# Splitting one inner token sum: the third raw row of T2 becomes an instruction of its own, placed just ahead of the other four rows

## The chip, the cores and the metric

The kernel runs on one core of a Trainium2 chip, in one launch. The metric is the device time of that core in microseconds, as the median over repeated executions. Five engines work side by side, each through its own queue in order: PE (TensorE, the matrix products), DVE (VectorE), ACT (ScalarE), POOL (GpSimd) and SP (SyncE, which here only issues DMAs). They wait for one another through semaphores.

## The reference, cut to what matters

Rows of 512 numbers (2 x 1024 of them) are normalized. A state-space convolution and a feed-forward net with low-rank additions are applied to the same normalized rows, and their product is added to the input. All numbers are float32.

```python
xn = layernorm(x)                                   # x: (2, 1024, 512)
s  = irfft(rfft(xn, 1024) * rfft(K, 1024))[..., :512] + D * xn
h1 = xn @ w1.T + 2 * (xn @ a1.T) @ b1.T             # hidden size 1376, rank 16
h3 = xn @ w3.T + 2 * (xn @ a3.T) @ b3.T
g  = silu(h1) * h3
f  = g @ w2.T + 2 * (g @ a2.T) @ b2.T
out = x + s * silu(f)
```

The change lies in the stage that makes h1 and h3, near its start.

## The kernel before, in words

**Tiling.** The 2048 tokens are cut into four blocks of 512, and a pair of blocks is a "sb" (there are NSB = 2). The products with w1 and w3 are done by a fast scheme with seven products in place of eight, applied twice: an outer level over quarters of the operands and an inner level over quarters of these. So 49 products of 128 x 128 by 128 x 512 make one pair of hidden chunks, and there are five pairs (NPAIR) and a remainder. The scheme wants sums of the operands. `outer_token_sum` makes the four outer sums T1 to T4 of the tokens for each sb into `xt`; the three quarters that enter unchanged stay in `xr`, the "raw" ones. `inner_token_sum` then makes the inner sums out of the raw quarters (3 rows of 512) and out of the outer sums (4 rows of 512). The inner T3 goes into tile `t_in[7]`, T2 into `t_in[6]`, T4 into `t_in[4]`, each with 7 rows: rows 0 to 2 raw, rows 3 to 6 from `xt`. T1 is made in place in `xr` and `xt`. All these sums are DVE work, with both inputs in SBUF. T3 is b22 - b12, T2 is T3 + b11, T4 is b21 - T2, so T2 needs T3 of the same rows.

**Who reads them.** A `Chain` is the run of seven inner-order products of one j (L766 on). Step i of chain j takes row `B_AT[i]` of the tile that belongs to j: T2's tile for j = 6, T3's tile for j = 7. The first chain with j = 6 stands at base 28 and takes its steps at the places `AT_T2`: step 1 (row 0) at 29.9, step 2 (row 1) at 33, step 6 (row 4) at 34.3, step 7 (row 5) at 34.8, step 5 (row 3) at 36.6, step 3 (row 2, the third raw row) at 39 and step 4 (row 6) at 43. `product` (L756) issues the matmuls; each float32 product of 512 columns stands as two MATMUL records in the trace. PE writes to four pairs of PSUM banks, `x`, `y`, `w` and `aux`. A bank is free again when ACT has copied it (L776, L794) or DVE has read it: L780 adds a `y` bank to a copy in SBUF, L870 adds a `x` or `w` bank to a running sum (`plus`). The same `plus` for the other half of the results, and the product of the gate (L837), run on POOL with all operands in SBUF. SP stores the finished gates to DRAM (L808).

**What sets the order.** Nothing is scheduled by a tool: the order is written out by hand. `at(place, what)` puts a call into a heap with a place; the heap is emptied in the order of the places (then in the order in which the calls came), and each call appends its instructions to its engine's queue. A place is about one product of 512 columns. `after(delay, what)` does the same relative to the place now being worked off. So a place decides what stands before what on each queue, and no more than that; the waits decide the times.

The list of inner token sums with their places stands at L1087 to L1098. The parameter `half` cuts a sum into two rows at a time and was used for T1 and T4 over `xt` only.

Of the kernel before, what the change touches and what calls it, by code (L numbers as in the profile page):

```python
# [107 lines left out]
def s4_gated_ffn(  # L108
# [107 lines left out]
    def at(place, what):  # L216
        heapq.heappush(events, (place, next(count), what))
# [116 lines left out]

    def inner_token_sum(name, raw, half=None):
        src, lo, n = (xr, 0, 3) if raw else (xt, 3, 4)
        some = slice(n) if half is None else slice(2 * half, 2 * half + 2)
        to = {i: t[:, lo : lo + n, :][:, some] for i, t in t_in.items()}
        b11, b21, b12_, b22 = (src[:, some, s, k, :] for s in range(2) for k in range(2))
        if name == 3:  # L340
            nc.vector.tensor_tensor(to[7], b22, b12_, sub)
        elif name == 2:
            nc.vector.tensor_tensor(to[6], to[7], b11, add)  # L343
        elif name == 4:
            nc.vector.tensor_tensor(to[4], b21, to[6], sub)
        else:
            nc.vector.tensor_tensor(b12_, b12_, b11, sub)
# [738 lines left out]
        at(when, lambda name=name: inner_weight_sum(w_pair[0], s_pair[0], name))  # L1086
    for name, raw, when, *half in (  # L1087
        (3, True, 21.6),
        (2, True, 22.8),
        (3, False, 24.2),  # L1090
        (2, False, 30.2),
        (1, True, 34.4),
        (1, False, 37.5, 0),
        (1, False, 40.3, 1),
        (4, True, 47.6),
        (4, False, 50.2, 0),
        (4, False, 52.3, 1),
    ):  # L1098
        at(when, lambda of=(name, raw, *half): inner_token_sum(*of))
# [495 lines left out]
```

## Time and profile before

| what | value |
|---|---|
| median of 3 runs | 442.54 us (442.51 to 442.62) |
| profiled execution | 442.84 us, of which the span is 441.0 us |
| mean granted TensorE clock | 0.998 |
| PE busy | 434.3 us, 98% of the span |
| DVE busy | 317.6 us, 72% |
| POOL busy | 207.9 us, 47% |
| ACT busy | 144.3 us, 33% |
| T2 raw (L343, 128x1536) | starts at 52.79 us, takes 2.64 us |
| T2 over `xt` (L343, 128x2048) | starts at 59.34 us, takes 2.27 us |

The span runs from the first to the last instruction; the profiled execution's time is 1.84 us longer than its span. A line of the timeline or of a group gives the engine, the line of the kernel, the operation, output<-inputs and shapes. "idle before <-" says what ended the engine's idle time. "PEld" is the load of weights into TensorE, which runs ahead of the product that needs it. A busy time includes time in which an instruction has started and is kept from its operands. On POOL the times are rough.

### The profile page before, as it was taken

What the parts mean: (1) busy time and instruction counts of PE and PEld (TensorE: products, weight loads), DVE (VectorE), ACT (ScalarE), POOL (GpSimd) and SP (SyncE); (2) the same over time, 40 slices, a digit from 0 to 9 for tenths busy, and PEclk for the clock granted to TensorE, in tenths of its full rate; (3) what the DMA queues carried; (4) which work ended last, traced back from release to release, by engine and by line L of the source; (5) the groups of instructions that cost most, each with busy time, mean ns of one, the idle gap of its engine ahead of it and who ended that gap; (6) DMA issues with size and microseconds to landing.
All of it is one profiled execution on the core that took longest, in us unless ns stands there. A gap on an engine that the chain in (4) does not pass through costs nothing.

```text
span 441.0 us, 5158 instructions
## 1 busy us (share of the span) xinstructions
PE 434.3 (98%) x1704; PEld 269.1 (61%) x1704; DVE 317.6 (72%) x536; ACT 144.3 (33%) x296; POOL 207.9 (47%) x156
## 2 busy tenths in 40 slices
PE   7999999999999999999999999999999999999996
PEld 7645334344444444444443446888898999999996
DVE  5899999954974687469745796979786885653234
ACT  2777242453255324532453242211101212212221
POOL 1416468895689368946894468400000122222221
PEclk9999999999999999999999999999999999999999
DMA  8931304025102500250035526395901832422211
GB/s 242 364 83 44 124 0 149 10 84 159 36 24 80 159 24 25 88 170 25 25 129 206 162 94 214 94 364 189 344 33 71 296 129 95 144 97 95 77 67 48
DMA packets 35467, 53.61 MB, mean 122 GB/s; under 512 B 4689, under 2 KB 21521, under 8 KB 35313
## 3 DMA queue, kind: packets, MB, share of 16 engines
q1 hardware_dynamic: 35088, 52.69, 36.3%
q10 hardware_dynamic: 352, 0.60, 0.4%
q8 instruction: 13, 0.21, 0.2%
q14 instruction: 14, 0.11, 0.1%
HBM read 33.88 MB, written 19.40 MB: 121 GB/s over the span
## 4 chain that ended last, share of the span: by engine, by line
PE 86%; DVE 7%; DMA 2%; ACT 2%; issue 1%; POOL 0%; SPq 0%; DVEq 0%; ACTq 0%; POOLq 0%
PE x L756 43%; PE y L756 22%; PE w L756 11%; PE aux L930 4%; PE w L930 2%; DMA s<-in_x_dram 1%; DVE xt L328 1%; DVE s L453 1%; DVE w L441 1%; DMA w<-in_w1T_dram 1%; PE y L529 1%; PE aux L711 1%; DVE t_in L343 1%; ACT c L254 1%; DVE aux L1310 1%
## 5 line engine op out<-in xcount | busy, mean ns | idle before, releaser
L1313 POOL TENSOR_TENSOR o<-o,xin 128x512 f32<-128x512 f32 (+1 forms) x17 | 23.3, 1369 | 133.0 <-DVE o L1312 133.0
L837 POOL TENSOR_TENSOR s<-c,s 128x512 f32<-128x512 f32 (+1 forms) x44 | 63.2, 1442 | 17.6 <-ACT c L829 12.4
L776 ACT COPY s<-x 128x512 f32<-128x512 f32 (+1 forms) x54 | 31.5, 584 | 84.5 <-PE x L756 84.4
L756 PE MATMUL x<-t_in,s 128*128 128x512 f32 (+1 forms) x148 | 55.4, 501 | 0.0
L870 POOL TENSOR_TENSOR s<-ua_three,s 128x512 f32<-128x512 f32 x20 | 35.9, 1793 | 25.4 <-DVE s L780 25.4
L780 DVE TENSOR_TENSOR s<-s,y 128x512 f32<-128x512 f32 (+1 forms) x54 | 36.0, 679 | 15.7 <-PE y L756 10.6
L756 PEld LDWEIGHTS x<-t_in,s 128*128 128x128 f32 x148 | 26.6, 190 | 23.3 <-issue 11.7
L870 POOL TENSOR_TENSOR ua_three<-ua_three,s 128x512 f32<-128x512 f32 x20 | 30.6, 1529 | 13.8 <-DVE s L780 13.8
L756 PE MATMUL y<-t_in,s 128*128 128x256 f32 (+1 forms) x108 | 35.9, 459 | 0.1
L1335 ACT COPY z<-x 128x256 f32<-128x256 f32 x24 | 8.8, 371 | 70.5 <-PE x L756 70.4
L870 POOL TENSOR_TENSOR s<-u_three,s 128x512 f32<-128x512 f32 x20 | 29.4, 1474 | 1.8 <-ACT c L829 1.0
L1310 DVE TENSOR_TENSOR aux<-aux,m 128x384 f32<-128x384 f32 x32 | 18.1, 565 | 15.8 <-PE aux L930 14.3
L829 ACT ACTIVATE c<-c 128x512 f32<-128x512 f32 x40 | 25.2, 632 | 12.9 <-DVE c L870 12.9
L756 PEld LDWEIGHTS y<-t_in,s 128*128 128x128 f32 x108 | 20.1, 190 | 11.6 <-issue 8.1
L794 ACT COPY w<-x 128x512 f32<-128x512 f32 (+1 forms) x37 | 21.1, 570 | 11.6 <-PE x L756 11.5
L870 POOL TENSOR_TENSOR u_three<-ua_three,u_three 128x512 f32<-128x512 f32 x10 | 15.6, 1556 | 13.4 <-DVE u_three L780 13.3
L756 PE MATMUL x<-t_in,w 128*128 128x512 f32 x40 | 21.0, 605 | 0.0
L756 PE MATMUL x<-xt,w 128*128 128x512 f32 x40 | 20.7, 598 | 0.0
L756 PE MATMUL x<-xr,w 128*128 128x512 f32 x40 | 20.6, 614 | 0.0
L756 PE MATMUL x<-xr,s 128*128 128x512 f32 x40 | 20.5, 614 | 0.0
L756 PE MATMUL x<-xt,s 128*128 128x512 f32 x40 | 20.4, 592 | 0.0
L756 PE MATMUL y<-xt,w 128*128 128x512 f32 x40 | 19.8, 592 | 0.0
(302 smaller groups left out, 908.7 us busy)
## 6 DMA issues: line engine op xcount, KB each, us to landing
g_dram<-s SPq DMA_DIRECT2D x40, 256.0 KB, 2.1
g<-g_dram SPq DMA_DIRECT2D x10, 512.0 KB, 5.8
xin<-in_x_dram SPq DMA_DIRECT2D x16, 256.0 KB, 2.7
out_dram<-o SPq DMA_DIRECT2D x14, 256.0 KB, 2.0
t_in<-g_dram SPq DMA_DIRECT2D x6, 512.0 KB, 4.1
w<-in_w1T_dram SPq DMA_DIRECT2D x10, 256.0 KB, 3.6
w<-in_w3T_dram SPq DMA_DIRECT2D x10, 256.0 KB, 4.9
t_in<-in_x_dram SPq DMA_DIRECT2D x8, 256.0 KB, 5.7
```

The lines of the kernel that those rows point to most:

```text
L254: nc.scalar.activation(value("c"), x_in[b][tt], AF.Copy, accum_out=sums_of_x[b][:, 0, tt : tt + 1])
L756: nc.tensor.matmul(ps[:, cols], lhsT=lhsT, rhs=rhs if parts == 1 else rhs[:, cols], start=first and i == 0 and part == 0, stop=i == len(pa ...
L776: nc.scalar.copy(t, self.x)
L780: nc.vector.tensor_tensor(t, t, self.y, add)
L794: nc.scalar.copy(self.w, self.x)
L829: nc.scalar.activation(c, c if src is None else src, AF.Silu)
L837: nc.gpsimd.tensor_tensor(g, act, g, mult)
L870: (nc.vector if o < 20 else nc.gpsimd).tensor_tensor(to, a, b, add)
L930: nc.tensor.matmul(to[:, n * P : (n + 1) * P], lhsT=x_, rhs=by, start=start, stop=True, skip_group_check=True,)
L1310: nc.vector.tensor_tensor(y[:, P:], y[:, P:], m[:, n * P : (n + 3) * P], add)
L1313: (nc.vector if last else nc.gpsimd).tensor_tensor(o, o, self.xin[h][:, cols], add)
L1335: nc.scalar.copy(t, xb)
```

## The change

The T2 sum of the raw rows was one DVE instruction over rows 0 to 2 (128x1536) at place 22.8. It is now two: rows 0 and 1 (128x1024) at 22.8 and row 2 (128x512) at 30.1, ahead of T2 over `xt` (rows 3 to 6) at 30.2. `half` is bounded so that the second half of three rows is one row.

```diff
     def inner_token_sum(name, raw, half=None):
         src, lo, n = (xr, 0, 3) if raw else (xt, 3, 4)
-        some = slice(n) if half is None else slice(2 * half, 2 * half + 2)
+        some = slice(n) if half is None else slice(2 * half, min(2 * half + 2, n))
         to = {i: t[:, lo : lo + n, :][:, some] for i, t in t_in.items()}
...
     for name, raw, when, *half in (
         (3, True, 21.6),
-        (2, True, 22.8),
+        (2, True, 22.8, 0),
         (3, False, 24.2),
+        (2, True, 30.1, 1),
         (2, False, 30.2),
         (1, True, 34.4),
```

On DVE's queue the order around it was and is:

| before | after |
|---|---|
| T3 raw, 128x1536 (L341) | T3 raw, 128x1536 |
| T2 raw, 128x1536 (L343) | T2 raw rows 0 and 1, 128x1024 |
| c<-ua_one,x (L870) | c<-ua_one,x |
| T3 over xt, 128x2048 (L341) | T3 over xt, 128x2048 |
| s<-s,y 128x512 (L780) | s<-s,y 128x512 |
| | T2 raw row 2, 128x512 |
| s<-s,y 96x512 (L780) | s<-s,y 96x512 |
| T2 over xt, 128x2048 (L343) | T2 over xt, 128x2048 |
| s<-w, 128x896 (L453) | s<-w, 128x896 |

The order on PE, ACT, POOL and SP is the same in both kernels.

## The prediction

> **What bounds the kernel now.** I read the share of each engine first (PE busy for 98% of the span, so it bounds the whole), then the chain of work that ended last around the change, then the timelines of DVE, POOL and PE there. A mean hides stages; the chain, in order of time, shows who set the pace here:
>
> ```profile
> 52.79 2.64 DVE t_in L343
> 55.42 0.61 DVE c L870
> ...
> 57.27 1.96 PE x L756 x4
> ```
>
> Up to 56.03 the chain is DVE, with the instruction that is split in it (2.64 us); two short steps of ACT follow, and from 57.27 PE carries it. DVE's own timeline, with the neighbours of the split instruction:
>
> ```profile
> 50.94 1.74 DVE L341 TENSOR_TENSOR t_in<-xr 128x1536 f32<-128x1536 f32 x1
> 52.79 2.64 DVE L343 TENSOR_TENSOR t_in<-t_in,xr 128x1536 f32<-128x1536 f32 x1
> 55.35 0.67 DVE L870 TENSOR_TENSOR c<-ua_one,x 128x512 f32<-128x512 f32 x1
> 55.95 2.28 DVE L341 TENSOR_TENSOR t_in<-xt 128x2048 f32<-128x2048 f32 x1
> 58.15 1.27 DVE L780 TENSOR_TENSOR s<-s,y 128x512 f32<-128x512 f32 x2
> 59.34 2.27 DVE L343 TENSOR_TENSOR t_in<-t_in,xt 128x2048 f32<-128x2048 f32 x1
> ```
>
> There is no gap over 0.11 us from 50.94 to 61.61: DVE is full (busy 6.00 of 6.00 us from 56 to 62). So T2 over xt, last of the list, ends when all the work ahead of it is done, in whatever order. POOL, at the same time:
>
> ```profile
> 48.69 5.12 POOL L870 TENSOR_TENSOR s<-ua_three,s 128x512 f32<-128x512 f32 x1 [6.04 <-DVE s L780]
> 58.90 4.86 POOL L870 TENSOR_TENSOR s<-ua_three,s 128x512 f32<-128x512 f32 x1 [5.09 <-DVE s L780]
> ...
> 73.46 1.27 POOL L870 TENSOR_TENSOR u_three<-ua_three,u_three 128x512 f32<-128x512 f32 x1
> ```
>
> The same operation takes 1.27 us alone and about 5 beside DVE's sums with both inputs in SBUF; DVE pays too, when POOL is in first: T2 raw took 2.64 us and T3 raw, of the same size, 1.74, so 0.90 of it was a wait until POOL's operation ended (48.69 + 5.12 = 53.81). I call that a collision. Last, PE:
>
> ```profile
> 56.08 1.13 PE L756 MATMUL x<-t_in,s 128*128 128x512 f32 x2
> 57.27 1.96 PE L756 MATMUL x<-xr,last 128*96 128x512 f32 x4
> 59.06 1.02 PE L756 MATMUL w<-t_in,s 128*128 128x512 f32 x2
> 59.92 1.88 PE L756 MATMUL y<-xt,last 128*96 128x512 f32 x4
> 61.67 1.12 PE L756 MATMUL x<-t_in,s 128*128 128x512 f32 x2
> 62.64 0.59 PE L756 MATMUL y<-t_in,s 128*128 128x512 f32 x1
> ```
>
> A product (two passes) takes 0.86 us from start to start (59.06 to 59.92). From 54.26 to 62.64 there are nine, 7.74 us, in 8.38: PE lost 0.64 us, at 56.08 (weights waited for c L870, which frees an x bank), at 57.27 (for ACT's copy, behind the silu of that c) and at 61.67 (for T2 over xt). Later, from 81.69 to 87.42, six products (5.16 us) took 5.73: another 0.57, again behind DVE (c L870 at 81.91, then L780). These two numbers, 1.21 together, are what PE can win here.
>
> **The change, part by part.**
>
> *The first piece.* Row to row, 512 elements more cost (2.28 - 0.67) / 3 = 0.54 us. The piece of 1024 starts at 52.79 behind the same T3 raw and the same POOL operation, so I keep the collision of 0.90: 2.64 - 0.54 = 2.10, ending 0.54 earlier. Bounds: 1.21 without a collision (as L345 128x1024 at 82.51), 2.64 if all is lost again. c L870, T3 over xt and the first L780 move up 0.54 with it; the products that these read ended before 52, so nothing new holds them. PE gains at 56.08 and 57.27 what those two waits cost, some 0.5 of the 0.64.
>
> *The piece that is moved.* Row 2 alone stands after that L780, at 58.15 - 0.54 = 57.61 + 0.60 = 58.21, and takes 0.67, with the next start 0.60 later (58.15 to 58.75). Between ends far apart, 0.6 and 0.6 + a collision of up to 1.74 (below), I take 0.60: what it overwrites in its tile POOL and PE had done with before T3 raw began, and POOL's next operation is released by the L780 just ahead, so it starts 0.1 behind this piece. What is queued behind it: the 96x512 L780 at 58.75 becomes 58.81 (+0.06, the fixed cost of one more instruction: 0.60 - 0.54). That L780 must end before PE may add to its y bank at 59.92: PE had its weights loading at 59.49, right as it ended (59.42). So PE's 0.5 is taken back to about 0.3 already here. The reader of row 2, step 3 of the chain, comes after steps 6, 7 and 5, all of which need T2 over xt, so the later row delays nobody. No DMA, and nothing on PE, ACT, POOL or SP, changes its place.
>
> *T2 over xt.* It starts at 59.41 instead of 59.34. Does it collide? Before, POOL's operation was released by the L780 at 58.15 and started at 58.90; T2 still ran in 2.27, without a collision, and POOL waited (4.86). After, POOL starts at about 58.37, while row 2 holds DVE; when row 2 ends at 58.81 the PSUM-reading L780 runs, and POOL can take its turn. The nearest rows are these:
>
> ```profile
> 78.10 1.08 DVE L453 TENSOR_TENSOR s<-w 128x896 f32<-128x896 f32 x1
> 79.10 0.67 DVE L780 TENSOR_TENSOR s<-s,y 128x512 f32<-128x512 f32 x1
> 79.70 1.69 DVE L345 TENSOR_TENSOR t_in<-xt,t_in 128x1024 f32<-128x1024 f32 x1
> ...
> 82.51 1.21 DVE L345 TENSOR_TENSOR t_in<-xt,t_in 128x1024 f32<-128x1024 f32 x1
> ```
>
> SBUF sum, L780, SBUF sum, with POOL's operation started at 78.32 inside the first: the second sum took 1.69 for 1.21, a collision of 0.48. I take 0.48: T2 takes 2.75, ends at 62.16 instead of 61.61, and PE's product of 61.67 starts at 62.22: +0.55, all earlier gain gone. Bounds: no collision, +0.06; the largest in the stretch, L347 128x1024 at 69.31, 2.95 for 1.21, so 1.74: +1.80.
>
> The Trainium skill, SBUF — State Buffer, "Who interferes with whom", says that a DVE instruction with two SBUF inputs and a GpSimd instruction that reads SBUF exclude each other, and that whichever issues first keeps the pair for the whole instruction. The 0.90 and 0.48 agree; the row at 59.34 does not by its start, since POOL's record begins 0.44 earlier and yet T2 ran free. By the rule the split opens a turn for POOL, and the sum is +0.55 at 62 us; by the row at 59.34 it is +0.06.
>
> *What becomes of the 0.55.* DVE stays full until 72.2, so it carries the 0.55 on. At 75.28 the raw T4 (L345 128x1536) took 2.29 for 1.74, waiting 0.55 for the POOL operation of 74.69 (end 75.95). POOL paces itself there (73.46, 74.69 back to back), so DVE coming 0.55 later finds it over: DVE is back at its old times from 77.5 on, but for some hundredths. PE, 0.55 late, then reaches 81.69 to 87.42, where it used to lose 0.57 to DVE, and loses nothing. Cover: this wait. Without it 0.55 stays. From 92 on DVE is idle for two thirds (3.44 us busy of 92 to 102), and PE carries the chain again.
>
> Sum on the profiled execution: +0.55 at 62, -0.49 to -0.55 by 87, so +0.00 to +0.06 on 442.84 (span 441.0 plus 1.84 around it). The median, 442.54, is 0.30 lower than that execution; the same step gives 442.6.
>
> **The rivals.**
>
> *B, DVE keeps its turn.* As at 59.34: no collision, T2 over xt only 0.06 later, everything after as before: 442.6. It differs in the trace, not in the time.
>
> *C, the 0.55 is not given back.* POOL's operations at 73.46 and 74.69 wait for L780s that are 0.55 late too; if they slide along, L345 collides as before, and PE keeps +0.55 to +0.61: 443.1. Against it: POOL was still waiting its turn when these L780s ended.
>
> *D, slower: POOL takes two turns.* At 69.31 L347 waited while two POOL operations passed. If L837, queued behind L870, passes ahead of T2 over xt as well, the collision is 1.74: PE +1.80 at 62, L345 gives back 0.55, leaving 1.25: 443.8. It decides from a collision of 0.88 + 0.55 - 0.06 = 1.37 on. Against it: that L837 reads what the L870 ahead writes, so it must wait for its end and leaves a gap to DVE.
>
> *E, faster: the collisions fall away.* If the shorter first piece is not held by POOL (0.90 of 2.64), DVE is up to 1.4 earlier from 54 on, T2 over xt can end ahead of PE, and so can c L870 and the L780s at 82 to 87: all of the 1.21, 441.3. Against it: POOL then takes its turn behind the piece, at c L870, and T3 over xt pays.
>
> **How the numbers follow.** My forecast (A, 0.48; 442.3 to 443.0 by itself) is 442.6. B 0.10, C 0.10, D 0.20, E 0.12: D and E get more than their arguments alone, since who is first is decided by tenths of a microsecond and every later turn hangs on it. 0.2% is 0.885 us, about what a measurement of this kernel can tell from no change. A, B and C lie within it (0.68), less 0.02 of A on each side: same 0.64, slower 0.22, faster 0.14. The range reaches up to D, 443.8, and down to 441.9, short of E; about 0.17 is left out.
>
> **What would show it.** L343 128x1024 about 2.1 us; c L870 at 54.8; L343 128x512 near 58.2, 0.67 long; POOL's L870 starting near 58.4 and lasting about 1.7 instead of 4.86; T2 over xt 2.75 us (2.27 says B, over 3.6 says D); PE's product behind it at 62.2; L345 128x1536 shorter than 2.29 (unchanged says C); the PE waits near 82 to 87 smaller. I am wrong if the shift at 62 differs from the shift at 100 by something other than these two, or if blocks behind 130 us, whose order did not change, run differently.

## The result and the profile after

| | median | lowest to highest | executions |
|---|---|---|---|
| before | 442.27 us | 441.78 to 442.88 | 13 |
| after | 443.61 us | 442.35 to 444.87 | 13 |

The ratio is 1.0028, with a 95% interval of 1.0018 to 1.0039. The kernel became slower by about 0.3%; the interval excludes no change, and its lower end, 0.18%, lies just under the prediction's bound of 0.2%. 443.61 lies inside the predicted range (441.9 to 443.8), but the likeliest single time was 442.6, no change, and "slower" had a chance of 0.22.

The profiled execution of the changed kernel took 443.06 us, with a span of 441.3 us and a mean granted clock of 0.999 (before: 442.84, 441.0, 0.998). Up to 54 us its instructions stand 0.15 us earlier than those of before, because the start of the span fell otherwise (PE's product of 54.26 is at 54.11). All shifts below have this 0.15 taken out; the shift of that product is what is taken out for the other kernels too. A "turn" of POOL below is one operation of POOL that goes between two sums of DVE while DVE's next sum, already started, stands still.

DVE's timeline of the changed kernel (start, duration, engine, line, operation, shapes, idle time before):

```profile
52.63 2.10 DVE L343 TENSOR_TENSOR t_in<-t_in,xr 128x1024 f32<-128x1024 f32 x1
54.66 0.67 DVE L870 TENSOR_TENSOR c<-ua_one,x 128x512 f32<-128x512 f32 x1
55.26 2.28 DVE L341 TENSOR_TENSOR t_in<-xt 128x2048 f32<-128x2048 f32 x1
57.46 0.67 DVE L780 TENSOR_TENSOR s<-s,y 128x512 f32<-128x512 f32 x1
58.06 0.68 DVE L343 TENSOR_TENSOR t_in<-t_in,xr 128x512 f32<-128x512 f32 x1
58.66 0.67 DVE L780 TENSOR_TENSOR s<-s,y 96x512 f32<-96x512 f32 x1
59.26 2.76 DVE L343 TENSOR_TENSOR t_in<-t_in,xt 128x2048 f32<-128x2048 f32 x1
61.94 2.15 DVE L453 TENSOR_TENSOR s<-w 128x896 f32<-128x896 f32 x1
...
70.76 1.74 DVE L347 TENSOR_TENSOR xt<-xt 128x1024 f32<-128x1024 f32 x1
...
74.90 0.69 DVE L870 TENSOR_TENSOR ua_one<-ua_one,w 128x512 f32<-128x512 f32 x1 [0.61 <-PE w L756]
...
76.10 1.75 DVE L345 TENSOR_TENSOR t_in<-xr,t_in 128x1536 f32<-128x1536 f32 x1
```

The first piece takes 2.10 us, row 2 0.68, T2 over `xt` 2.76: as forecast to 0.01. The line that the forecast lacks is the next one: the weight sum of L453 takes 2.15 us, where it took 1.07 before at 61.55. The rows of the kernel before to set beside these:

```profile
61.55 1.07 DVE L453 TENSOR_TENSOR s<-w 128x896 f32<-128x896 f32 x1
...
69.31 2.95 DVE L347 TENSOR_TENSOR xt<-xt 128x1024 f32<-128x1024 f32 x1
...
75.28 2.29 DVE L345 TENSOR_TENSOR t_in<-xr,t_in 128x1536 f32<-128x1536 f32 x1
```

POOL's timeline of the changed kernel says why:

```profile
58.21 1.65 POOL L870 TENSOR_TENSOR s<-ua_three,s 128x512 f32<-128x512 f32 x1 [4.56 <-DVE s L780]
59.95 10.23 POOL L837 TENSOR_TENSOR s<-c,s 128x512 f32<-128x512 f32 x4
```

Its L870 takes 1.65 us instead of 4.86 (the turn that costs T2 over `xt` 0.48), so the L837 queued behind it is ready at 59.95, in the middle of T2 over `xt`. When T2 ends, L837 goes next and L453 stands for 1.08 us. (The experiment without POOL's turns, below, tests this reading.)

POOL does not take more of DVE than before; it takes it earlier. What the sums of DVE lose to POOL between 58 and 78 us, each against the same shape without a collision:

| DVE's sum | before | after |
|---|---|---|
| T2 over xt (2.27) | 0 | 0.49 |
| L453 128x896 (1.07) | 0 | 1.08 |
| L347 128x1536 (1.75) | 0.48 | 0.47 |
| L347 128x1024, first (1.21) | 0.48 | 0.48 |
| L347 128x1024, second (1.21) | 1.74 | 0.53 |
| L345 128x1536 (1.74) | 0.55 | 0.01 |
| sum | 3.25 | 3.06 |

Two turns have moved from 69 to 76 us, where no product is waiting for DVE, to 59 to 63 us, where PE is. In DVE's timeline above, L347 at 70.76 (1.74 us instead of 2.95) and L345 at 76.10 (1.75 instead of 2.29) are the turns that are gone there, and at 74.90 DVE waits 0.61 us for PE: from there on DVE is late only because PE is. It is 0.97 late at 76.10 like PE, and 0.42 late from 77.77 on, since L345 no longer collides. PE's timeline of the changed kernel, around 62 us and then around 85 us:

```profile
62.07 1.13 PE L756 MATMUL x<-t_in,s 128*128 128x512 f32 x2 [0.73 <-DVE t_in L343]
63.04 1.02 PE L756 MATMUL y<-t_in,s 128*128 128x512 f32 x2
64.24 1.95 PE L756 MATMUL x<-t_in,s 128*128 128x512 f32 x4 [0.18 <-DVE s L453]
```

```profile
82.50 1.02 PE L756 MATMUL x<-xt,s 128*128 128x512 f32 x2
83.36 1.02 PE L756 MATMUL x<-t_in,w 128*128 128x512 f32 x2
84.22 1.10 PE L756 MATMUL x<-xr,s 128*128 128x512 f32 x2
...
86.88 1.02 PE L756 MATMUL y<-t_in,w 128*128 128x512 f32 x2
87.74 1.02 PE L756 MATMUL y<-xt,s 128*128 128x512 f32 x2
```

And the same five products in the kernel before:

```profile
81.69 1.02 PE L756 MATMUL x<-xt,s 128*128 128x512 f32 x2
82.64 1.13 PE L756 MATMUL x<-t_in,w 128*128 128x512 f32 x2
83.77 1.12 PE L756 MATMUL x<-xr,s 128*128 128x512 f32 x2
...
86.45 1.12 PE L756 MATMUL y<-t_in,w 128*128 128x512 f32 x2
87.42 1.02 PE L756 MATMUL y<-xt,s 128*128 128x512 f32 x2
```

PE is 0.55 us late at 62.07 (62.07 - 61.67 + 0.15) and, after the wait for L453, 0.97 late from 65 to 82.50. The 0.57 that the kernel before lost between 81.69 and 87.42 is nearly all gone (5.24 us for the six products instead of 5.73), so at 87.74 PE is 0.48 late. It stays at 0.48 up to 105 us. This +0.48 is what the change does to the schedule; the engines' times up to 100 us repeat to 0.03 in a second profile of the same kernel.

Behind 100 us single profiles scatter. There, a load of weights from DRAM may end the chain (the shift falls to 0.11 at 107 us only because the kernel before lost 0.36 there in its profile). The experiments go into both parts.

### The profile page after: what moved, and what is told of

The parts are those of the page before. It is cut to its first block, busy times and chain, and to the rows that moved or that the text cites. A ratio compares the mean times of both kernels' runs of the same rounds, so it can differ in the third digit from the quotient of the medians.

```text
span 441.3 us, 5159 instructions
## 1 busy us (share of the span) xinstructions
PE 434.2 (98%) x1704; PEld 269.4 (61%) x1704; DVE 317.2 (72%) x537; ACT 144.4 (33%) x296; POOL 206.6 (47%) x156
## 4 chain that ended last, share of the span: by engine, by line
PE 85%; DVE 9%; ACT 2%; issue 2%; DMA 1%; POOL 0%; SPq 0%; DVEq 0%; POOLq 0%
PE x L756 43%; PE y L756 22%; PE w L756 11%; PE aux L930 4%; PE w L930 2%; DVE s L453 1%; DVE t_in L343 1%; DMA s<-in_x_dram 1%; DVE xt L328 1%; DVE t_in L341 1%; DVE w L441 1%; PE y L383 1%; PE y L529 1%; PE aux L711 1%; ACT c L254 1%
## 5 line engine op out<-in xcount | busy, mean ns | idle before, releaser
L837 POOL TENSOR_TENSOR s<-c,s 128x512 f32<-128x512 f32 (+1 forms) x44 | 66.1, 1508 | 16.7 <-ACT c L829 11.5
L780 DVE TENSOR_TENSOR s<-s,y 128x512 f32<-128x512 f32 (+1 forms) x54 | 36.0, 678 | 15.8 <-PE y L756 10.6
L870 POOL TENSOR_TENSOR s<-ua_three,s 128x512 f32<-128x512 f32 x20 | 32.7, 1634 | 25.1 <-DVE s L780 25.1
L870 POOL TENSOR_TENSOR ua_three<-ua_three,s 128x512 f32<-128x512 f32 x20 | 29.6, 1481 | 13.8 <-DVE s L780 13.8
L870 POOL TENSOR_TENSOR s<-u_three,s 128x512 f32<-128x512 f32 x20 | 29.4, 1473 | 1.8 <-ACT c L829 1.0
L870 POOL TENSOR_TENSOR u_three<-ua_three,u_three 128x512 f32<-128x512 f32 x10 | 15.6, 1556 | 15.8 <-DVE u_three L780 14.0
L756 PE MATMUL y<-xt,s 128*128 128x512 f32 x40 | 19.8, 592 | 0.0
```

The source lines that it names most:

```text
L756: nc.tensor.matmul(ps[:, cols], lhsT=lhsT, rhs=rhs if parts == 1 else rhs[:, cols], start=first and i == 0 and part == 0, stop=i == len(pa ...
L780: nc.vector.tensor_tensor(t, t, self.y, add)
L837: nc.gpsimd.tensor_tensor(g, act, g, mult)
L870: (nc.vector if o < 20 else nc.gpsimd).tensor_tensor(to, a, b, add)
```

## The experiments

Theory A: the loss is two turns of POOL that the new order brings forward, at T2 over `xt` and at L453. Rival X: one more instruction, standing at its own place, costs by itself. Rival Y: the loss comes from the load of weights near 101 us. In the shift table PE's starts stand against the kernel before, with the shift of the product at 54.26 taken out (us; the column heads are times in the kernel before):

| kernel | 58.2 | 62.6 | 64.8 | 87.0 | 105.2 |
|---|---|---|---|---|---|
| after | -0.46 | +0.55 | +0.97 | +0.48 | +0.48 |
| after again | -0.46 | +0.58 | +0.99 | +0.50 | +0.50 |
| split only | +0.09 | +0.09 | +0.09 | +0.10 | +0.10 |
| row 2 early | -0.46 | +0.09 | +0.09 | +0.10 | +0.10 |
| row 2 late | -0.46 | -0.51 | +0.52 | +0.03 | +0.04 |
| row 2 between | -0.46 | +1.16 | +1.16 | +0.67 | +0.67 |

**The same kernel again.**

> The changed kernel once more, with its profile, to see another execution of it. Theory A (turns): row 2 ends while GpSimd's addition is waiting, GpSimd takes the turn, T2 over xt takes 2.7 to 2.8 us, GpSimd takes the next turn ahead of s<-w (L453), which takes about 2.1 us instead of 1.07, and TensorE is 0.5 us late at 62 us and more after 64 us; how much of it is given back by 92 us differs from execution to execution. Time +0.2 to +0.4% against the kernel before. Rival X (the extra instruction itself costs): T2 over xt back at 2.27 us and the time as late all the same. Rival Y (a weight load from DRAM near 101 us): TensorE no later than before at 92 us and later behind 103 us.

443.12 us (442.12 to 444.38, 12 executions) against 442.52 (35) on the same chip: ratio 1.0015 (1.0003 to 1.0028). T2 over `xt` takes 2.76 and L453 2.15 again. So it is slower by 0.15 to 0.28%, on both sides of the bound of 0.2%. PE is 0.50 late at 87 and at 105 us, ahead of what waits for the load, so rival Y does not explain the schedule's part. The profiled execution was one of the long ones, 444.22 us, and its chain of waits shows where the rest was lost, in two stretches:

```profile
100.63 0.40 SPq L402
101.03 0.05 issue
101.08 4.96 DMA w<-in_w1T_dram
...
106.17 0.70 DVE w L393
106.87 0.04 issue
106.91 1.12 PE y L756 x2
...
228.83 9.31 DMA w_a<-in_w2T_dram
```

The load of w1 took 4.96 us (3.45 in the profile before), L393 waited for it, and PE for L393: PE lost 1.00 us there, and its shift goes from 0.50 to 1.13 (the kernel before lost 0.36 at the same place). The load of w2 took 9.31 us (8.46 to 8.91 in the other profiles), and the shift goes to 1.68. At 301 us it grows by another 0.2, behind a wait for DVE.

**The split alone.** Row 2 directly behind rows 0 and 1:

```diff
-        (2, True, 30.1, 1),
+        (2, True, 22.81, 1),
```

> Row 2 is split off but stands right behind rows 0 and 1 (place 22.81). Theory A: the two pieces follow each other without a turn for GpSimd, T2 over xt keeps 2.27 us, everything from there on is 0.07 us later, so the time is 0.0 to +0.1 us. Rival X: as late as the change, +1.0 to +1.5 us. Rival Y: no statement, unless the load near 101 us moves.

442.39 us (441.75 to 443.87, 12), ratio 0.9998 (0.9987 to 1.0008). DVE's timeline of it:

```profile
58.95 2.28 DVE L343 TENSOR_TENSOR t_in<-t_in,xt 128x2048 f32<-128x2048 f32 x1
61.15 1.08 DVE L453 TENSOR_TENSOR s<-w 128x896 f32<-128x896 f32 x1
```

The additional instruction costs PE 0.09 us and no measurable time. No turn of POOL falls at T2 over `xt` or at L453.

**The move, but to an earlier place**, behind T3 over `xt` and ahead of the first L780:

```diff
-        (2, True, 30.1, 1),
+        (2, True, 24.3, 1),
```

> Row 2 stands behind T3 over xt (place 24.3), ahead of the L780 that releases GpSimd, so GpSimd starts in the PSUM-reading L780 as before and not in an SBUF sum. c<-ua_one,x still moves up by 0.54 us. Theory A: T2 over xt keeps 2.27 us, 0.07 us later than before; time 0.0 to +0.1 us. Rival X: +1.0 to +1.5 us. If moving c<-ua_one,x up does harm by itself, +1.0 us or more with T2 over xt at 2.27 us.

442.47 us (442.06 to 443.23, 12), ratio 0.9996 (0.9988 to 1.0005). Here c L870 and T3 over `xt` come 0.52 earlier, about as in the changed kernel (PE -0.46 at 58.2), row 2 stands by itself, and T2 over `xt` takes 2.28 and L453 1.08. Rival X falls with these two runs: split and moved apart, the row costs nothing as long as POOL's turns stay where they were.

**The move to a later place**, behind T2 over `xt`:

```diff
-        (2, True, 30.1, 1),
+        (2, True, 30.25, 1),
```

> Row 2 stands behind T2 over xt (place 30.25), its reader comes later still. Theory A: GpSimd's start falls in the second L780 as before, T2 over xt keeps 2.27 us and ends 0.5 us earlier than before, TensorE's product behind it starts about 0.4 us earlier, and from s<-w (L453) on everything on VectorE is 0.07 us later, which by 87 us sets TensorE again: time -0.1 to +0.1 us. Rival X: +1.0 to +1.5 us.

442.30 us (441.75 to 443.87, 12), ratio 0.9994 (0.9983 to 1.0005). T2 over `xt` is free, as expected, but a turn falls on row 2 behind it, which was not expected; DVE's timeline:

```profile
58.35 2.28 DVE L343 TENSOR_TENSOR t_in<-t_in,xt 128x2048 f32<-128x2048 f32 x1
60.56 1.76 DVE L343 TENSOR_TENSOR t_in<-t_in,xr 128x512 f32<-128x512 f32 x1
62.25 1.08 DVE L453 TENSOR_TENSOR s<-w 128x896 f32<-128x896 f32 x1
```

One turn (1.08 us) makes PE 0.52 late at 65 us, and PE gives back 0.49 of it by 87: what the prediction said of one turn, nearly to the hundredth (+0.03).

**Two neighbours of the changed kernel exchanged**, so that row 2 stands between the second L780 and T2 over `xt`:

```diff
-        (2, True, 30.1, 1),
+        (2, True, 30.15, 1),
```

> The changed kernel with two neighbours on DVE exchanged: row 2 behind the second L780 (96x512) instead of ahead of it, so the order is L780, L780, row 2, T2 over xt. Theory A (what decides is when POOL's L870 gets its first turn, and so where the turn of L837 falls): POOL waits inside the second L780 as before; either it gets no turn until T2 over xt and L453 are done (T2 over xt 2.27, L453 1.07, PE at 86 us +0.0 to +0.1, ratio 1.000), or it gets one at row 2 (row 2 about 1.75, T2 over xt free, PE +0.55 at 62, no second turn at L453 unless L837 is ready by its end; at 86 us 0.0 to +0.5). Rival X (a row of its own at this place costs by itself): as the changed kernel, PE +0.48 at 86 us, ratio 1.002 to 1.003.

442.75 us (442.20 to 443.18, 11) against 442.21 (21): ratio 1.0007 (0.9998 to 1.0016). DVE's timeline:

```profile
58.38 1.77 DVE L343 TENSOR_TENSOR t_in<-t_in,xr 128x512 f32<-128x512 f32 x1
60.07 2.28 DVE L343 TENSOR_TENSOR t_in<-t_in,xt 128x2048 f32<-128x2048 f32 x1
62.27 1.08 DVE L453 TENSOR_TENSOR s<-w 128x896 f32<-128x896 f32 x1
```

POOL gets a full turn at row 2 (1.77 for 0.68, so 1.09), and none at T2 over `xt` or L453. PE waits 1.49 us for T2 and is 1.16 late:

```profile
62.40 1.12 PE L756 MATMUL x<-t_in,s 128*128 128x512 f32 x2 [1.49 <-DVE t_in L343]
```

The 1.77 was expected, the 1.16 not: I had added a turn of 0.48 for PE, where a row of 1.77 means one of 1.09, and 0.06 + 1.09 is the 1.15 measured to 0.01. The give-back is again 0.49, which leaves +0.67. So one turn can cost PE more than the two of the changed kernel, if all of it falls on the sum that PE waits for next.

**POOL's turns taken away, in both kernels.** The five operations of POOL from 58 to 71 us work on 16 of 512 columns; the rest of these additions and gate products is left out, so only the schedules are compared, one profile of each:

```diff
-                    nc.gpsimd.tensor_tensor(g, act, g, mult)
+                    n = 16 if 25 < now[0] < 38 else TB
+                    nc.gpsimd.tensor_tensor(g[:, :n], act[:, :n], g[:, :n], mult)
...
+            if o >= 20 and 25 < now[0] < 38:
+                to, a, b = to[:, :16], a[:, :16], b[:, :16]
```

> The kernel before, with POOL's five operations of this stretch (the L870 addition on s and the gate products of L837 from 58 to 71 us) done on 16 of their 512 columns, so that POOL hardly takes a turn; the rest of those additions and products is left out, and its time is that of a kernel that leaves them out. It is the base for after_small_pool, profile against profile. Every theory: T2 over xt 2.27 us, s<-w L453 behind it 1.07, L347 128x1024 about 1.21 in place of 2.95, so DVE up to 1.7 us earlier from 70 us on and PE's waits from 82 to 87 us smaller than before's 0.57.

> The changed kernel with the same five POOL operations on 16 of 512 columns (the same part left out). Theory A (the loss is two turns that POOL takes at T2 over xt and at L453): both turns gone, T2 over xt 2.27 to 2.35, L453 1.07 to 1.15, and PE at 64 us and at 86 us within 0.1 us of before_small_pool. Rival X (the extra instruction and the new order of DVE cost by themselves, whatever POOL does): PE still 0.4 us or more behind before_small_pool at 64 and at 86 us.

DVE's timeline of the changed kernel with the small operations (L873 is the L870 of the other kernels):

```profile
58.79 2.28 DVE L343 TENSOR_TENSOR t_in<-t_in,xt 128x2048 f32<-128x2048 f32 x1
60.99 1.08 DVE L453 TENSOR_TENSOR s<-w 128x896 f32<-128x896 f32 x1
61.99 0.68 DVE L873 TENSOR_TENSOR ua_one<-ua_one,w 128x512 f32<-128x512 f32 x1
62.59 1.75 DVE L347 TENSOR_TENSOR xr<-xr 128x1536 f32<-128x1536 f32 x1
```

Both turns are gone. PE's shift against the kernel before is +0.07 at 65 us and -0.42 at 87 for this one, +0.01 and -0.47 for its base, so the change is worth +0.06 and +0.05 between the two. That is theory A's number, and the fixed cost of one instruction; rival X wanted 0.4 or more. The base shows besides what POOL's turns cost the kernel before in this stretch: 0.47 us by 87 us (441.96 and 441.51 us were the single times of the two).

**The loss near 85 us, taken away alone.** In the kernel before, the next pair's first weight sum (L453 at 78.10) is put later:

```diff
-                (3, ready(7) + 1.2),
+                (3, ready(7) + (14 if c == 0 else 1.2)),
```

> The kernel before with one other instruction moved: the next pair's first weight sum (L453 128x896 at 78.10 us, 1.0 us of DVE) goes behind 92 us, where DVE is idle for two thirds. If PE's loss of 0.57 us from 81.69 to 87.42 is DVE being late there, as the prediction has it, PE is 0.4 to 0.57 us earlier at 87 us and the time is 442.0, ratio 0.9985 to 0.999. If that loss comes from elsewhere (ACT, or the banks themselves), PE is unchanged at 87 us and the ratio 1.000. The sums that follow s7 come later with it; if PE then waits for them behind 95 us, the gain is lost there.

PE's timeline of it, where the kernel before needs 5.73 us for the six products:

```profile
81.13 1.02 PE L756 MATMUL x<-xt,s 128*128 128x512 f32 x2
81.99 1.02 PE L756 MATMUL x<-t_in,w 128*128 128x512 f32 x2
...
86.37 1.02 PE L756 MATMUL y<-xt,s 128*128 128x512 f32 x2
```

It needs 5.24, and PE is 0.47 us earlier: that loss is DVE being late, as the prediction had it. The gain does not last. 443.17 us (442.75 to 443.73, 11), ratio 1.0019 (1.0010 to 1.0029): slower, where 442.0 was expected. By 96 us 0.30 of the 0.47 is gone, and I read that from the timeline as the later weight sums standing ahead of the additions to `y`; at 106.41, in this profile, PE's `y` product waits 0.97 behind a load of weights of 4.96 us (shift +0.70). The first I had named as a risk, the second not. Whether that load is what makes the other ten executions slow too, one profile does not show.

**What is behind 100 us.** The medians of the changed kernel are 1.34 and 0.60 us above before's, the schedule explains 0.48. In the next three kernels the merge of the next pairs' weights, which waits for the loads, stands two products later:

```diff
-                at(t0 + 15.6, step(merge_whole_pair))
+                at(t0 + 17.6, step(merge_whole_pair))
```

> The kernel before with the merge of the next pair's weights (the four products of L383 at 102.6 us and the L393 behind them, which wait for the load w<-in_w1T of 100.6) put two products, 1.7 us, later; no wait of PE for that L393 should be left near 106 us. Theory L (part of every time of this kernel is how long that load takes, 3.4 to 5.0 us in the profiles): 0.2 to 0.5 us faster than before and less spread. Otherwise (the load's wait is rare): ratio 1.000.

> The changed kernel with the same merge 1.7 us later. The changed kernel's median has been 0.6 to 1.3 us above before's, and the turns of POOL explain 0.48 of it by 86 us. Theory L (the rest is longer waits for the weight load, which its DVE order does not set by itself): 0.4 to 0.6 us above before_merge_later, all of it there by 86 us. Rival Z (the rest is lost elsewhere, behind 107 us, whatever the load does): 0.9 us or more above before_merge_later.

> Row 2 on its own directly behind c L870 (PE 0.27 us earlier than before by 107 us) with the merge 1.7 us later. If both gains hold and add: 0.3 to 0.7 us faster than before, ratio 0.9985 to 0.9993. If they are the same wait told twice: as before_merge_later.

| kernel | median | lowest to highest, executions | ratio to before |
|---|---|---|---|
| before, on this chip | 442.55 | 441.78 to 443.96, 27 | |
| before, merge later | 442.77 | 442.30 to 443.23, 11 | 1.0005 (0.9996 to 1.0013) |
| after, merge later | 443.10 | 442.78 to 444.58, 11 | 1.0015 (1.0003 to 1.0028) |
| row 2 early, merge later | 442.80 | 442.13 to 443.56, 11 | 1.0006 (0.9997 to 1.0014) |

With the merge later, the two kernels differ by 0.33 us in the median and by 0.52 in the mean (443.27 - 442.75). In their profiles the difference is 0.46 us at 87 and at 107, 0.47 at 239 and 0.82 at the end; the last 0.35 comes behind 239 us, where the order of neither kernel differs. That speaks against rival Z (0.9 or more) and, less clearly, for theory L (0.4 to 0.6): the mean fits it, the median lies below, and not all of the profiles' difference is there by 86 us. The other half of L's expectation failed: with the later merge the kernel before ranges less widely (442.30 to 443.23 instead of 441.78 to 443.96, but in 11 executions against 27) and is not faster, so no cost of the load's wait was saved there. No gain adds up in the third kernel either, and no version that I ran beats the kernel before.

Taken together, the schedule costs 0.48 us. The changed kernel's lowest times fit that: over its two sets the tenth percentile of its 25 executions is 442.41 us, that of the 48 of the kernel before measured with them 441.94, so +0.47. Its upper end is further away (ninetieth percentile 444.31 against 443.19, +1.12). That a long execution is one with long loads is shown in one profile (the 444.22 us above); with the merge later one of the changed kernel's eleven still took 444.58. Why the changed kernel should meet more long executions is open.

## Why the prediction was right and where it failed

- **The first piece**: right. 2.10 us with the collision kept at 0.90, c L870 0.54 earlier, PE 0.46 earlier at 58.2 (forecast some 0.5).
- **The moved piece**: right. 0.60 on DVE, nothing paid for its own place, PE's gain back to 0.30 at 60.4 (forecast 0.3).
- **T2 over xt**: right, with its mechanism. POOL starts at 58.21, takes the turn when row 2 ends, T2 takes 2.76 and PE's product is 0.55 late. Of the two readings set against each other there, the one from the Trainium skill, SBUF — State Buffer, "Who interferes with whom" (the pair is held for a whole instruction by whichever issues first), gave +0.55, and that is what was measured. The rule alone does not give it: with row 2 behind T2 POOL's record also begins first (57.91, T2 at 58.35), as in the kernel before (58.90, 59.34), and T2 ran free in 2.28.
- **What becomes of the 0.55**: here it failed. The give-back itself came as described: L345 took 1.75 instead of 2.29, and PE's loss near 85 us shrank by 0.49 (forecast 0.49 to 0.55). But the sum took T2's collision for the only one. The operation that follows on POOL, L837, became ready about 3.8 us earlier, since L870 ended that much earlier (59.86 instead of 63.76), and its turn fell at the end of T2, on L453: 1.08 us on DVE, 0.42 on PE. +0.55 + 0.42 - 0.49 is the +0.48 that stands there in place of +0.00 to +0.06. DVE, which the sum had back at its old times from 77.5 on, is 0.42 late there.
- **Rival D** had that very operation in hand and dropped it for a reason that was half right: L837 must wait for L870's end, so it could not pass ahead of T2 over `xt`. It passed behind it instead. D priced one place for the second turn; the next boundary between two sums was not looked at.
- **Rival B** was refuted by the 2.76. **C** has nearly the measured number (+0.55 to +0.61 kept, +0.48 measured) without the mechanism: C's L345 was to collide as before, and it did not. **E** is far off.
- **Blocks behind 130 us**: no cost of the change shows there; what differs most between profiles behind 100 us is how long PE waits for loaded weights. The prediction reckoned with one profiled execution and did not allow for this scatter. The schedule is 0.48 us longer, the medians are 0.60 and 1.34 higher; the rest is not accounted for.
- **The range**: that 443.61 lies within it is in part luck. Its upper end was set by D's +1.25, whose collision (1.74 at T2) did not come; the +1.34 measured is 0.48 of schedule and 0.86 for which the prediction had no term.

## What to carry to other kernels

When an engine off the critical path shares something with the one that is full, list its next two or three queued operations and the time at which each becomes ready after the change, and put each to the next boundary, not only the first. A change can leave the sum of such collisions as it was (3.25 and 3.06 us here) and still cost time, by bringing them forward to where the bounding engine waits. A give-back later on is bounded by what was lost there before (0.57 us here): the first 0.5 us of lateness was free, the next 0.5 was not.

## What the runs showed of the hardware that was not expected

- Who goes next between two sums of DVE that follow one another is not settled by who waited longer. In the kernel before POOL waited from 58.90 and did not get the boundary between T2 over `xt` and L453 at 61.6; in the changed kernel it waited from 59.95 and got the same boundary; with row 2 behind T2 it waited from 57.91 and got the boundary between T2 and row 2. There was no gap on DVE in any of the three, and the first and the third had waited about as long (2.7 us). What decides it is open.
- An operation of POOL on 16 of 512 columns took 0.60 us where it had its turn, but 3.80 us in the base kernel (58.60 to 62.40): a small operation too can wait for microseconds when DVE's sums follow one another.
- The second of two loads of 256 KB of weights, issued at 100 to 102 us, took between 3.06 and 3.71 us in eleven of the thirteen profiles and 4.96 us in two (the changed kernel again and the later weight sum), where PE lost 1.00 and 1.24 us. The kernel before lost 0.36 us at this place although its load took 3.45 us: SP's two issues took 1.78 us there, not the 0.97 of the changed kernel, so the load began later.
